# When the first scores start: eight maxima instead of eleven ahead of them

## The chip, the cores and the metric

The kernel runs on one core of a Trainium2 chip. The metric is device time in microseconds (us), the median of three runs. A core has TensorE (PE in the profile; PEld are its weight loads), VectorE (DVE), ScalarE (ACT), GpSimd (POOL) and SyncE (SP). Each works through its own queue in program order. SP issues most DMAs; ACT and POOL can issue some, and issuing takes their time.

## The reference

Input is x, 8 rows (B) of 512 tokens by 128 features, in float32. Each row is layer-normed (no learned scale) to xn. The output is x plus two things computed from xn:

- Differential attention with 8 heads. Queries and keys of each head have two halves of 8 features, values have 16. For each half: softmax of q·k / sqrt(8) over the row's 512 tokens. The second half's attention times diff_weight is taken from the first's, the result weighs the values, is rms-normed per token over all heads, scaled by norm_w, and goes through Wo; then bo and a factor 1 − diff_weight.
- A mixture of experts. A gate (xn @ Wg, sigmoid) picks 2 of 8 experts per token, with shares normed to one. Each expert is silu(xn @ We1) * (xn @ We3) @ We2 with 256 inner features; one shared expert of that kind takes all tokens. The sum is divided by 3.

## The kernel before, in words

A row is 4 tiles of 128 tokens. Its 8 heads are taken in 4 pairs (w). A pair needs first its *maxima*: for each of the two heads and each tile of queries, a product of queries and keys (L795), 128 by 1024 numbers in PSUM for the two halves together, and a reduction over them on VectorE (L802). So a pair has eight maxima. Then `shift` (L825 to 838) turns the eight maxima of each token into rows that go by DMA into the queries (`into_queries`, L820), so that the scores come out with the maximum already taken off. For the very first pair this goes through a transpose on TensorE (pm, L829), a copy on ScalarE (first_rows, L831) and two DMAs on SP.

*Scores* (L844) are the same products the other way round, with keys in the rows; ScalarE takes exp of them (L852), and `weigh` (L863) multiplies by the values, with a column of ones for the sums. Scores, maxima and weigh have a PSUM buffer each (tags "sc", "mx", "av"); only the first pair's maxima use "sc" too, by turns. Other products share three buffers (tag "mm").

The main loop has 16 steps for a row, 128 in all, plus some; a step is one pair and one tile of keys and has two turns, one for each head of the pair. A turn issues scores, then one tile of maxima (`next_maxima(1)`) for a pair to come, then at most one of the waiting DMA jobs (`copies`, `loads`, `errands`). The maxima run ahead of the scores by a fixed number of tiles: 11 are made before the loop (AHEAD), and one more is put in at the first turn, so that from there on the lead is 12. 

Everything else is cut into pieces, which generators yield with a cost in us of TensorE and a number of PSUM buffers. `pieces(step)` starts them in the first turn of a step, by due date (last step less pieces left), while the room of 2.25 us and the free buffers allow. What stands behind "soon" and "late" in a generator follows in that turn or the next. These jobs matter here:

- `norm_later(b)`: layer norm of row b (rows 0 to 2 are normed ahead of the loop): statistics on VectorE (L213 to 217), the rest on GpSimd (L218, L222).
- `gates_later`: for each row turn(b), four transposes (px, L236) and a copy to xnT (L270), then in the next piece gates(b), four products (pg, L249). Rows 0 and 1 are gated ahead of the loop. When all rows are gated, the exponential of the gates (L274) lets `route()` start, which picks experts and lists the tokens of each, in more than 20 pieces, mostly on VectorE. The experts' pieces wait for it.
- `prepare(b)`: queries and keys (pq, L727), split in an upper and a lower part (L738, L740), then values (pv, L771). The parts are copied by DMA into the places in qst and kst that the products read (L758); each such job is one entry of `copies`, two DMAs.

Ahead of the loop the order is written out by hand (L1071 to L1173): norm of row 0, the weights' transposes (pw, L1090), px of row 0, `head` for the queries and keys of the first pair (pd, L1118, without a DMA), row 0's other heads by prepare(0) and 16 DMAs, and the first eleven maxima. Between the maxima stand the gates of rows 0 and 1, and `keep_clock()` (L1149), a product of the unit matrix with xnT whose result nobody reads: ten of them. One product of 512 float32 columns is two instructions in the trace.

Of the kernel before, what the change touches and what calls it, by code (L numbers as in the profile page):

```python
# [11 lines left out]
F32 = mybir.dt.float32  # L12
# [19 lines left out]
def kernel(  # L32
# [52 lines left out]
    nc = tc.nc  # L85
    B, S, E = x.shape
    NT = S // P
    NE, _, FF = We1.shape
# [19 lines left out]
    def small_psum(name):  # L108
        return ps_3.tile([P, S], F32, tag="mm", name=name)
# [68 lines left out]
    kst = []  # L178
# [53 lines left out]
    def turn(b):  # L232

        px = small_psum(f"px_{b}")
        for t in range(NT):
            nc.tensor.transpose(px[:, t * P : (t + 1) * P], xn[b][:, t, :], ident)  # L236
        xnT = p3.tile([P, S], F32, tag="xnT", name=f"xnT_{b}")
        return xnT, px
# [4 lines left out]
    def gates(b, xnT):  # L243

        if not pgs:
            pgs.append(small_psum("pg"))
        for t in range(NT):
            i = b * NT + t
            nc.tensor.matmul(  # L249
                pgs[0][:, i * NE : (i + 1) * NE], xnT[:, t * P : (t + 1) * P], wg, start=True, stop=True  # L250
            )

    def norm_later(b):
        yield 0, 0
        yield "late"
        run(norm(b))

    def gates_later(rows):

        previous = None  # L260
        for b, ready_at in rows.items():
            while step < ready_at:
                yield 0, 0
            yield 1.35, 1
            if previous:
                gates(*previous)
            xnT, px = turn(b)
            previous = b, xnT
            yield "late"
            nc.scalar.copy(xnT, px)  # L270
        yield 0.9, 0
        gates(*previous)
        yield "late"
        nc.scalar.activation(  # L274
            gate.rearrange("p t e -> p (t e)"), pgs[0][:, : TILES * NE], AF.Exp, scale=-1.0
        )
        held.pop()
        gated.append(True)
# [266 lines left out]
    turns = 0  # L545
# [169 lines left out]
    def prepare(b):  # L715

        st = state[b]
        if "xnT" not in st:
            yield 0.45, 1
            st["xnT"], px = turn(b)  # L720
            yield "late"
            nc.scalar.copy(st["xnT"], px)
        xnT = st["xnT"]
        yield 1.75, 2
        pqs = [small_psum(f"pq_{b}_{i}") for i in range(2)]
        for i in range(2):
            nc.tensor.matmul(  # L727
                pqs[i],
                w_c[:, i].rearrange("p i f u -> p (i f u)") if b else w_rest[:, i],
                xnT,  # L730
                start=True,
                stop=True,
            )
        parts = []
        for i in range(2):
            yield ("soon", "late")[i]
            upper = p1.tile([P, S], F32R, tag=f"upper{i}", name=f"upper_{b}_{i}")
            nc.scalar.copy(upper, pqs[i])  # L738
            lower = p1.tile([P, S], F32R, tag=f"lower{i}", name=f"lower_{b}_{i}")
            nc.vector.tensor_tensor(lower, pqs[i], upper.bitcast(F32), ALU.subtract)  # L740
            parts.append((upper, lower))
        q, k = qst[b % 2], kst[b % 2]

        def no_shift():
            for half in range(2):
                nc.sync.dma_start(
                    out=q[64 * half + SHIFT : 64 * half + SHIFT + 2]
                    .bitcast(F32)
                    .rearrange("p u s -> p (u s)"),
                    in_=noughts,  # L750
                )

        def copy(part, i, s):

            row_of = (2 * part + s, part + 2 * s)[i]
            first = 0 if b else 2
            for half in range(2):
                (nc.scalar if b == 0 and i else nc.sync).dma_start(  # L758
                    out=(q, k)[i][64 * half + row_of : 64 * half + STACK : 4, first:, :].bitcast(F32),
                    in_=parts[i][part][64 * half : 64 * half + F * (H - first), :].bitcast(F32),  # L760
                )

        if b > 1:
            copies.append(no_shift)
        for part, i in ((0, 0), (0, 1), (1, 0), (1, 1)):
            for s in range(2):
                copies.append(lambda part=part, i=i, s=s: copy(part, i, s))
        yield 0.9, 1
        pv = small_psum(f"pv_{b}")
        for t in range(NT):  # L770
            nc.tensor.matmul(  # L771
                pv[:, t * P : (t + 1) * P],
                xnT[:, t * P : (t + 1) * P],
                w_t[:, 0, :],
                start=True,
                stop=True,
            )
        yield "late"
        nc.scalar.copy(
            vals[b % 2].rearrange("p t h e -> p (t h) e")[:, :, 0:DH],  # L780
            pv.rearrange("p (n e) -> p n e", e=DH),
        )
# [182 lines left out]


    STEPS = 4 * NT
    AHEAD = 11
    MIX = 30
    EACH = 4.65  # L970
    ROOM = 2.25
# [14 lines left out]
    def job(first, last, pieces, part, ready=None):  # L986

        jobs.append(Job(first, last, pieces, part, ready or (lambda: True)))

    for b in range(3, B):  # L990
        job(b - 3, b - 3, 1, norm_later(b))
    job(1, 7, 7, gates_later({b: b - 1 for b in range(2, B)}))
    job(5, 24, 22, route(), lambda: gated)
    for b in range(B):
        at = STEPS * b
        st = state[b]
        if b == 1:
            job(0, 1, 2, prepare(b))
        elif b > 1:
            job(at - 16, at - 15, 3, prepare(b))  # L1000
        job(at + 5, at + 13, 2, shared(b), lambda b=b: len(over) == b)
        job(at + 3, at + 4, 1, residual(b))
        for w in range(4):
            job(at + 4 * w + 5, at + 4 * w + 6, 1, fold(b, w), lambda st=st, w=w: ("ov", w) in st)
        job(at + 12, at + 18, 1, shared_out(b), lambda st=st: "h" in st and "r" in st)
        job(at + 17, at + 21, 2, conclude(b), lambda st=st: st.get("folds") == 4 and "r" in st)
# [55 lines left out]
    with tc.manual_schedule():  # L1062
# [3 lines left out]

        norms = {b: norm(b) for b in range(B)}
        next(norms[0])  # L1070
        rows = const.tile([P, 5], F32, name="rows")  # L1071
# [13 lines left out]
            nc.vector.tensor_scalar(signs[:, i : i + 1], lower, -2.0, 1.0, ALU.mult, ALU.add)  # L1085
        run(norms[0])

        pw = ps_1.tile([P, S], F32, tag="av", name="pw")
        for i in range(4):
            nc.tensor.transpose(pw[:, i * P : (i + 1) * P], w_raw[:, i, :], ident)  # L1090
# [51 lines left out]
            w = pw[:, i * P : (i + 1) * P]  # L1142
            nc.scalar.copy(w_c[:, i], w.rearrange("p (u i f) -> p i f u", i=2, f=F))
        nc.scalar.copy(w_t.rearrange("p i e -> p (i e)"), pw[:, 2 * P :])

        idle = ps_1.tile([P, S], F32, tag="av", name="idle")

        def keep_clock():
            nc.tensor.matmul(idle, ident, xnT, start=True, stop=True)  # L1149

        next_maxima(1)
        state[1]["xnT"], px = turn(1)
        nc.scalar.copy(state[1]["xnT"], px)
        keep_clock()
        next_maxima(1)
        run(first)
        while copies:
            copies.popleft()()
        later_constants()
        next_maxima(1)  # L1160
        gates(0, xnT)
        keep_clock()
        next_maxima(1)
        gates(1, state[1]["xnT"])
        held.append(pgs[0])
        keep_clock()
        next_maxima(1)
        keep_clock()
        next_maxima(1)
        for _ in range(AHEAD - 8):  # L1170
            keep_clock()
            next_maxima(1)
            keep_clock()  # L1173
        sides = const.tile([P, 1], F32, name="sides")
        nc.vector.memset(sides, 1.0)
# [42 lines left out]
        while step < total + 1 or jobs or errands or loads:  # L1218
            for second_half in range(2):
                if step < total:  # L1220
                    b, r = divmod(step, STEPS)
                    w, c = divmod(r, NT)
                    pe = scores(b, w, c, second_half)
                    pes = [pe] if not second_half else pes + [pe]
                if shifted:
                    shifted.popleft()()
                next_maxima(1)
                turns += 1
                if errands:

                    if latest:
                        nc.gpsimd.tensor_copy(mark, latest.pop())  # L1232
                    errands.popleft()()

                if copies and (turns % 3 or not loads):
                    copies.popleft()()
                elif loads:
                    loads.popleft()()
                if not second_half:
                    begun = pieces(step)  # L1240
                    if turns <= 1:
                        next_maxima(1)
                    follow(begun, "soon")
                else:
                    follow(begun, "late")
                    if last is not None:
                        weigh(*last)
                    if turns <= 1:
                        next_maxima(1)
                    last = (b, w, c, pes) if step < total else None  # L1250
            step += 1
# [48 lines left out]
```

## Time and profile before

| | |
|---|---|
| three runs | 671.24, 671.82, 671.85 us, median 671.82 |
| the profiled execution | 684.2 us, of which the span is 682.3 |
| TensorE busy | 625.5 us, 92% of the span |
| VectorE busy | 518.2 us, 76% |
| ScalarE busy | 357.5 us, 52% |
| mean granted TensorE clock | 0.954 |
| first scores (L844) | 46.22 us after the span's start |
| step 7 of the loop begins | 81.14 us |
| last scores | 668.55 us |

The span runs from the first to the last instruction. In an answer in order of time, a line gives start, duration, engine, line of the code, operation, what it writes and reads, and in brackets how long the engine had been idle and what released it. "SPq" and "ACTq" are DMAs issued by these engines. In an answer by stretches, a line gives the stretch, its length, then the busy time of PE, PEld, DVE, ACT and POOL, each with a count of instructions, then the granted clock of TensorE (PEclk), the busy share of the DMA engines and GB/s.

### The profile page before, as it was taken

How to read it: one execution, taken by the hardware profiler on the slowest of the kernel's cores; microseconds unless marked ns; L12 is line 12 of the kernel's file. 1: busy time of each engine (PE TensorE's matmuls, PEld its weight loads, DVE VectorE, ACT ScalarE, POOL GpSimd, SP SyncE). 2: the span in 40 equal slices, each digit the busy share in tenths (PEclk: the TensorE clock that was granted, in tenths of full speed). 3: DMA queues.
4: the chain of work that ended last, by engine and by line, in shares of the span. 5: the costliest groups of instructions: out<-in, count | busy, mean ns of one | idle time of the engine just before them, and what ended most of it. 6: DMA issues, size and time to landing. Idle time of an engine off the chain costs nothing.

```text
span 682.3 us, 10940 instructions
## 1 busy us (share of the span) xinstructions
PE 625.5 (92%) x3781; PEld 329.0 (48%) x3781; DVE 518.2 (76%) x945; ACT 357.5 (52%) x435; POOL 278.7 (41%) x455
## 2 busy tenths in 40 slices
PE   4988998789998999999999999999999999999874
PEld 1424543245543554556555554455555655555222
DVE  7658658997778787767777777867778687778983
ACT  2214543453445655566555655656466655555552
POOL 7516600048704144544544444553445425523101
PEclk9978867796989999999999999999999999999997
DMA  5222332021500233435462234435353234401360
GB/s 168 75 89 69 117 105 95 26 73 59 155 26 22 72 97 122 153 115 161 127 181 86 85 121 136 148 122 155 119 188 92 100 98 149 121 18 30 131 220 33
DMA packets 41665, 72.64 MB, mean 106 GB/s; under 512 B 10581, under 2 KB 15862, under 8 KB 41586
## 3 DMA queue, kind: packets, MB, share of 16 engines
q1 hardware_dynamic: 35978, 61.05, 28.2%
q0 software_dynamic: 4608, 9.45, 4.8%
q10 hardware_dynamic: 1024, 1.44, 0.7%
q8 instruction: 30, 0.49, 0.3%
q14 instruction: 25, 0.20, 0.1%
HBM read 46.19 MB, written 12.60 MB: 86 GB/s over the span
## 4 chain that ended last, share of the span: by engine, by line
PE 70%; DVE 21%; issue 5%; ACT 3%; POOL 0%; DVEq 0%; ACTq 0%; POOLq 0%
PE sc L844 13%; PE av L863 13%; PE mx L795 10%; DVE most L802 10%; PE ph L632 8%; PE py L645 5%; PE ps L885 3%; ACT pe L852 3%; PE ph L959 2%; PE pi L435 2%; PE po L903 2%; PE pq L727 2%; PE idle L1149 2%; PE pg L249 1%; PE pz L942 1%
## 5 line engine op out<-in xcount | busy, mean ns | idle before, releaser
L802 DVE TENSOR_REDUCE most<-mx 128x2 f32<-128x1024 f32 x256 | 312.8, 1222 | 107.4 <-PE mx L795 107.0
L852 ACT ACTIVATE pe<-sc 128x1024 f32<-128x1024 f32 x256 | 262.4, 1025 | 241.4 <-PE sc L844 239.5
L844 PE MATMUL sc<-qst,kst 64*128 64x512 f32 x512 | 131.6, 511 | 12.5 <-ACT pe L852 12.2
L863 PE MATMUL av<-pe,vals 128*32 128x512 f32 x1024 | 142.7, 630 | 0.0
L795 PE MATMUL mx<-kst,qst 64*128 64x512 f32 x512 | 123.1, 472 | 16.4 <-DVE most L802 14.5
L844 PEld LDWEIGHTS sc<-qst,kst 64*128 64x128 f32 x512 | 49.0, 188 | 157.4 <-ACT pe L852 115.7
L569 POOL DMA_INDIRECT xq<-tokens,tokens_at x72 | 71.1, 987 | 37.2 <-issue 27.0
L657 POOL DMA_INDIRECT results<-y,results_at x72 | 70.8, 984 | 36.5 <-issue 31.4
L795 PEld LDWEIGHTS mx<-kst,qst 64*128 64x128 f32 x512 | 51.4, 193 | 62.2 <-DVE most L802 50.9
L1232 POOL COPY mark<-most 1x2 f32<-1x2 f32 x144 | 25.4, 176 | 136.8 <-DVE most L802 134.2
L632 PE MATMUL ph<-xT,w 128*128 128x128 f32 x576 | 74.8, 281 | 1.0 <-DVE r L946 0.9
L632 PEld LDWEIGHTS ph<-xT,w 128*128 128x128 f32 x576 | 67.6, 191 | 9.3 <-issue 6.6
L914 POOL TENSOR_TENSOR o<-on 128x128 f32<-128x128 f32 x32 | 14.8, 462 | 137.8 <-DVE on L910 137.7
L863 PEld LDWEIGHTS av<-pe,vals 128*32 128x32 f32 x1024 | 20.6, 109 | 43.0 <-issue 42.8
L645 PE MATMUL py<-w,h 128*128 128x128 f32 x288 | 38.4, 283 | 2.8 <-DVE h L609 2.8
L645 PEld LDWEIGHTS py<-w,h 128*128 128x128 f32 x288 | 33.9, 191 | 8.0 <-issue 4.1
L606 DVE SCALAR_TENSOR_TENSOR th<-th,ph 128x512 f32<-128x512 f32 x36 | 24.6, 685 | 14.1 <-ACT th L605 14.1
L885 PE MATMUL ps<-xnT,s 128*128 128x512 f32 x64 | 32.1, 620 | 0.6 <-DVE on L910 0.6
L605 ACT ACTIVATE th<-ph 128x512 f32<-128x512 f32 x36 | 21.5, 597 | 15.6 <-PE ph L632 13.7
L873 ACT ACTIVATE ov<-av,sides 128x512 f32<-128x512 f32 x32 | 22.2, 694 | 6.8 <-PE av L863 6.5
L609 DVE TENSOR_TENSOR h<-th,ph 128x512 f32<-128x512 f32 x36 | 24.1, 669 | 0.0
L222 POOL TENSOR_SCALAR xn<-xn,both,rstd 128x128 f32<-128x128 f32 x28 | 22.0, 797 | 0.7
(161 smaller groups left out, 600.3 us busy)
## 6 DMA issues: line engine op xcount, KB each, us to landing
w<-experts SPq DMA_DIRECT2D x72, 384.0 KB
ym<-results SPq DMA_DIRECT2D x16, 256.0 KB
qst<-upper SPq DMA_DIRECT2D x28, 128.0 KB
kst<-upper SPq DMA_DIRECT2D x28, 128.0 KB
qst<-lower SPq DMA_DIRECT2D x28, 128.0 KB
kst<-lower SPq DMA_DIRECT2D x28, 128.0 KB
experts<-in_L_ffn_We_dram SPq DMA_DIRECT2D x24, 128.0 KB
r<-in_L_attn_x_dram SPq DMA_DIRECT2D x8, 256.0 KB
```

The lines of the kernel that those rows point to most:

```text
L569: nc.gpsimd.indirect_dma_start(out=xq[:, n, :], out_offset=None, in_=tokens[:, :], in_offset=bass.IndirectOffsetOnAxis(ap=tokens_at[:, j : ...
L606: nc.vector.scalar_tensor_tensor(th, th, 1.0, ph, ALU.add, ALU.mult)
L632: nc.tensor.matmul(ph[:, ns], ws[n][:, f : f + P], xT[:, ns], start=True, stop=True)
L645: nc.tensor.matmul(py[:, ns], hs[c][:, ns], ws[n][:, f : f + E], start=(c == 0), stop=(c == NF - 1))
L657: nc.gpsimd.indirect_dma_start(out=results_of[j], out_offset=bass.IndirectOffsetOnAxis(ap=results_at[:, j : j + 1], axis=0), in_=y[:, n, : ...
L795: nc.tensor.matmul(sc[:, i, :], q[ROWS[i], 2 * w + u, t * P : (t + 1) * P], k[ROWS[i], 2 * w + u, :], start=True, stop=True,)
L802: nc.vector.tensor_reduce(most[:, t, u, :], sc, AX.X, ALU.max, negate=True)
L844: nc.tensor.matmul(sc[:, i, :], kst[b % 2][ROWS[i], 2 * w + u, c * P : (c + 1) * P], qst[b % 2][ROWS[i], 2 * w + u, :], start=True, stop=True,
L852: nc.scalar.activation(pe, sc, AF.Exp, scale=F**-0.5)
L863: nc.tensor.matmul(st["av"][32 * g : 32 * g + 32, :], vals[b % 2][:, c, 2 * w + u, :], pes[u][:, i, :], start=(c == 0), stop=(c == NT - 1),)
L885: nc.tensor.matmul(ph, w[:, c * P : (c + 1) * P], st["xnT"], start=True, stop=True)
L1232: nc.gpsimd.tensor_copy(mark, latest.pop())
```

## The change

- Maxima: eight, not eleven, are made before the loop; in the loop, turns 2, 3, 4 and 6 make one more each, instead of turn 1 alone. From turn 6 on the lead is again 12.
- Unit products: ten become seven. Two come at the very start, ahead of the weights' transposes, and read a part of kst that L184 has filled with ones; one stands between maxima 5 and 6, one between 7 and 8, three after the eighth.
- Gates: row 0's move one maximum later; row 1's move into the loop's gates job, which starts at step 2 instead of 1 and takes each row two steps later than before.
- Norms of rows 3 to 7 come at steps 2 to 6 instead of 0 to 4; prepare(1) at steps 1 and 2 instead of 0 and 1.
- Of the 16 DMAs of row 0's queries and keys, the four with the keys' upper part move from ACT's queue to SP's.

```diff
@@ gates_later
             if previous:
                 gates(*previous)
+            if b in state and "xnT" in state[b]:
+                previous = b, state[b]["xnT"]
+                continue
             xnT, px = turn(b)
@@ copy, in prepare
-                (nc.scalar if b == 0 and i else nc.sync).dma_start(
+                (nc.scalar if b == 0 and i and part else nc.sync).dma_start(
@@ 
-    AHEAD = 11
+    CATCH_UP = 2, 3, 4, 6
@@ jobs
     for b in range(3, B):
-        job(b - 3, b - 3, 1, norm_later(b))
-    job(1, 7, 7, gates_later({b: b - 1 for b in range(2, B)}))
+        job(b - 1, b - 1, 1, norm_later(b))
+    job(2, 9, 8, gates_later({b: b + 1 for b in range(1, B)}))
...
         if b == 1:
-            job(0, 1, 2, prepare(b))
+            job(1, 2, 2, prepare(b))
@@ ahead of the loop
+        idle = small_psum("idle")
+        some = kst[0][:, 2, :].bitcast(F32)
+
+        def keep_clock():
+            nc.tensor.matmul(idle, ident, some, start=True, stop=True)
+
         norms = {b: norm(b) for b in range(B)}
...
         run(norms[0])
 
+        for _ in range(2):
+            keep_clock()
         pw = ps_1.tile([P, S], F32, tag="av", name="pw")
...
         idle = ps_1.tile([P, S], F32, tag="av", name="idle")
-
-        def keep_clock():
-            nc.tensor.matmul(idle, ident, xnT, start=True, stop=True)
-
+        some = xnT
         next_maxima(1)
         state[1]["xnT"], px = turn(1)
         nc.scalar.copy(state[1]["xnT"], px)
-        keep_clock()
         next_maxima(1)
         run(first)
         while copies:
             copies.popleft()()
         later_constants()
         next_maxima(1)
-        gates(0, xnT)
         keep_clock()
         next_maxima(1)
-        gates(1, state[1]["xnT"])
+        gates(0, xnT)
         held.append(pgs[0])
-        keep_clock()
         next_maxima(1)
         keep_clock()
         next_maxima(1)
-        for _ in range(AHEAD - 8):
-            keep_clock()
-            next_maxima(1)
+        for _ in range(3):
             keep_clock()
@@ main loop, in both turns
-                    if turns <= 1:
+                    if turns in CATCH_UP:
                         next_maxima(1)
```

More of the change, by code (lines that the diff above doesn't have):

```diff
@@ L1247 @@
                         weigh(*last)
-                    if turns <= 1:
+                    if turns in CATCH_UP:
                         next_maxima(1)
```

## The prediction

> **What bounds the kernel now.** I read the page's head and slices first, then the chain of waits, then the first 80 us in order of time, then busy time and clock in stretches.
>
> ```profile
> span 682.3 us, 10940 instructions
> ...
> PEclk9978867796989999999999999999999999999997
> ...
> PE 70%; DVE 21%; issue 5%; ACT 3%; POOL 0%; DVEq 0%; ACTq 0%; POOLq 0%
> ```
>
> TensorE carries 70% of the chain, VectorE 21%. So work taken off TensorE counts only where TensorE is what the next step waits for; each stretch must be asked by itself. The change touches the stretch up to step 10 of the main loop (about 0 to 100 us). In order of time, around the first scores:
>
> ```profile
> 33.43 0.49 PE L795 MATMUL mx<-kst,qst 64*128 64x512 f32 x2
> 33.96 1.23 DVE L802 TENSOR_REDUCE most<-mx 128x2 f32<-128x1024 f32 x1 [0.25 <-PE mx L795]
> ...
> 35.71 0.17 DVE L809 TENSOR_TENSOR parts<-most,parts 128x8 f32<-128x8 f32 x1
> ...
> 35.93 0.39 PE L829 MATMUL pm<-ident,parts 128*32 128x128 f32 x1 [2.01 <-DVE parts L809]
> ...
> 36.12 1.92 PE L1149 MATMUL idle<-xnT,ident 128*128 128x512 f32 x2
> 36.36 0.26 ACT L831 COPY first_rows<-pm 32x128 f32<-32x128 f32 x1 [8.43 <-DMA kst<-lower]
> 36.64 1.37 SPq L820 DMA_DIRECT2D qst<-first_rows  x2
> ...
> 38.69 3.78 PE L1149 MATMUL idle<-xnT,ident 128*128 128x512 f32 x4
> ...
> 46.22 0.49 PE L844 MATMUL sc<-qst,kst 64*128 64x512 f32 x2
> ```
>
> The eighth maximum (33.43) ends the first pair; its shift is issued on SP from 36.64 to 38.01, and in quarter-microseconds the DMA share falls to 0.03 by 39.5 before the experts' loads begin, so the first scores could run from about 39.4. They run at 46.22, behind six unit products (x2 in the trace is one product) and three more maxima in TensorE's order. That is the gap the change closes: 6.8 us.
>
> In the loop, a tile of maxima has one PSUM buffer (tag "mx"), so matmul and reduction alternate:
>
> ```profile
> 60.16 1.22 DVE L802 TENSOR_REDUCE most<-mx 128x2 f32<-128x1024 f32 x1
> ...
> 61.98 1.22 DVE L802 TENSOR_REDUCE most<-mx 128x2 f32<-128x1024 f32 x1 [0.60 <-PE mx L795]
> 63.12 0.86 DVE L213 BATCH_NORM_STATS2 stats<-xn 128x6 f32<-128x128 f32 x4
> ```
>
> One maximum costs 1.22 plus 0.60 of waiting, 1.82 us, unless other VectorE work (here a norm's 0.86 + 0.36 + 0.17 = 1.4 us) fills the wait. VectorE is busy 28.6 of the 34.9 us of steps 0 to 6: this alternation sets the pace there. Whatever the change moves into these steps is paid at VectorE's price.
>
> The clock, on a grid of 3.41 us on which its changes fall:
>
> ```profile
> core 0: us, PE busy (x) PEld busy (x) DVE busy (x) ACT busy (x) POOL busy (x), PEclk, DMA share, GB/s
> ...
> 15.17:18.59 3.42, 2.97 (x6) 1.03 (x6) 1.62 (x2) 0.13 (x1) 3.32 (x5) 1.00 0.01 2
> 18.59:22.00 3.41, 3.41 (x6) 1.42 (x7) 1.89 (x3) 1.33 (x2) 3.41 (x2) 1.00 0.00 0
> ...
> 32.24:35.65 3.41, 1.68 (x6) 0.48 (x4) 2.84 (x5) 0.00 (x0) 0.00 (x0) 0.99 0.36 114
> 35.65:39.07 3.42, 3.14 (x6) 1.20 (x7) 0.44 (x3) 0.26 (x1) 0.00 (x0) 0.50 0.19 52
> ...
> 52.72:56.13 3.41, 3.41 (x16) 2.64 (x16) 2.83 (x10) 0.00 (x0) 2.17 (x3) 0.51 0.00 0
> ```
>
> A half-busy stretch (1.68 of 3.41) is followed by half clock; a wholly busy one ends it. The clock column reads 1.00 before 35 us only because no change is recorded: four pd products take 3.75 us there, about 0.94 each, against 0.5 after 22 us.
>
> **The change, step by step.**
>
> **A. Two unit products before the weights' transposes.** They read the ones that L184 writes, ready at 4.06. At the cold rate (3.78 us for two) they hold TensorE from 4.1 to 7.9. Behind them in its queue stand the four pw transposes (1.35 us; before, done by 6.4), now done at 9.2, and px of row 0, which ran 8.25 to 9.49. VectorE's four_rest copies (8.88) need the first two transposes, there at 8.6: no wait. If the clock stays cold, px slips by 0.9 us and so does all behind it: +0.9. If it rises, the pd products and the first pq run at half the time. By the Trainium skill (TensorE: Matmul & The Clock Gate, Part 1) one fully busy window of about 3.4 us suffices; its Part 4 says against the change that transposes do not count as busy, which would leave 3.8 us of products, rarely a whole window: +0.9. The row decides: 52.72 to 56.13, which brought the clock back, holds four px transposes (1.06 us) among its busy time. So from 4.1 to about 10 us there is, mostly, a whole window, and the clock rises at some point between 8 and 12. Rise at 8.4: pd from 10.3, maximum 1 at 14.15 instead of 15.62; then 11.8 to 15.2 is only half busy, the clock falls and returns as in 18.59 to 22.00, one window earlier; maximum 3 at 20.9 for 23.26, −2.4. Rise at 11.8: 21.6, **−1.7**. I take −1.7; bounds −3.2 (never falls again) to +0.9.
>
> **B. First scores behind the eighth maximum.** Between maxima 3 and 8 go two unit products and row 1's gates (1.12 + 1.10 + 1.06); there VectorE's 1.23 per reduction takes over as pace in part. Written out from 23.26: reductions 24.6, 25.8, 27.05, 28.35, 29.95, 31.55 for 33.96: −2.4. The upper part of k moves from ACT's queue to SP's: SP issues 12 copies at 0.73, from 23.15 to 31.9, then must take the shift at 34.2: 2.3 us of room. ACT's four take 3.98 from 26.9 to 30.9, before first_rows at 33.9 (with eight it would have been 34.9: the move is needed). All copies land by about 34, before maximum 9. After pm: six products and three maxima at full clock 6 × 1.0 + 3 × 0.5, 7.6 with gaps; instead, the longer of three products (3.0) and the shift (0.30 + 1.37 + about 1.4 to land, 3.2). −4.4. At the half clock of the profile: 9.9 against 3 × 1.89 = 5.7, −4.2. B: **−6.7**, either way.
>
> **C. Paid back in the loop.** Three more maxima in steps 0 to 2 (extra at turns 2, 3, 4, 6 for turn 1), written out with 1.02 for exp, 0.5 per product: reductions 9 to 18 end at 2.3, 4.1, 5.9, 7.7, 10.2, 12.2, 14.1, 16.0, 18.2 and 20.8 after the first scores (prepare's two lower parts 1.4, parts 0.9 and one norm in between), the nineteenth at 22.6. The same place before: 65.59 − 46.22 less 0.65 for the cold stretch at 53 to 56, 18.75. +3.85. Two norms that were done by then are not: 2 × (1.4 − 0.6 + 0.1 of gaps), +1.8. C: **+5.65**. Row 1's gates (1.06 of TensorE) lie under the alternation of steps 3 to 6, where TensorE has idle time; without that cover +1.06. VectorE's 0.8 us of sides and keep, in the loop's way at 46.45, now lie under the shift's flight; counted above.
>
> **D. Gates, row 1's queries, routing.** The planner's first gate piece with row 1 runs at step 4 and the last at step 10 instead of 8; routing starts and ends two steps later (30 instead of 28), the first expert at step 35 instead of 33. Two steps lose routing's VectorE work early and two gain it late; experts run three to five steps behind their dates anyway and the last ends near step 115, with nothing waiting until 118. Row 1's copies at steps 1 to 6 have until step 10. 0, bounds −1 to +1.
>
> **Sum:** −1.7 − 6.7 + 5.65 = −2.75. The profiled execution, 684.2 (682.3 span and 1.9 around it), would become 681.4. It is 12.4 above the median; it holds about 55 us of half clock before 200 us, so I carry the difference, not the level, to the median: 671.82 − 2.75 = **669.1**.
>
> **Rivals.**
> 1. *Slower: the clock falls in step 0.* The first 4.65 us after the new first scores have 2.5 us of products, 54%; the row at 32.24 fell at 49%. From there pq (2.0) and pv (1.06) double. One window costs up to 1.7 us where TensorE is the pace; from the second on the gain is gone. The profile has five in a row (80 to 97 us, each fully busy yet half clock); four would give −2.75 + 6.8 = +4, 675.9. Against: steps 1 and 2 have about 80% of work, and the kernel before risks the same (it fell at 52.7).
> 2. *No difference:* the early products only delay (A = +0.9) or C reaches 7: 671.8, within 1.3.
> 3. *Larger:* the clock stays up from 8 us (A = −3.2) and the extra maxima fill idle VectorE time. Counted by VectorE's idle time: from reduction 3 (24.59) to step 7 (81.14) it is busy 39.9 of 56.55 us; of the 16.6 idle, 2.3 (six products and three maxima at half clock) + 0.65 come from the clock, which leaves 13.7. After: 0.9 between reductions 3 and 8, 3.9 until reduction 9, nine unfilled waits of 0.6: 10.2. B and C give −3.5, with A −6.7: 665.1.
>
> **How the numbers follow.** 0.2% of the median, 1.3 us, is about what a measurement can tell from no change. Likeliest 0.45 (667.5 to 670.5); larger 0.12; none 0.20; slower 0.23. The first, but for 0.01, and the second are faster: 0.56; same 0.21; slower 0.23. The range goes from 665.0 to 676.0, taking in rival 1 to four windows.
>
> **What would show it.** Right: the first scores at 37 to 40 us; pd products at half their 0.94 before 16 us; reductions 10 to 18 at 1.82 apart; step 7 only two to four us earlier than its 81.1. Wrong: pd still 0.94 (A), SP issuing copies past 34 (B), PEclk 0.50 in steps 0 to 3 (rival 1), experts late past step 115 (D).

## The result, and the profile after

The changed kernel takes **678.99 us** (median of 4 runs, 678.57 to 682.60), the kernel before 671.84 us on the same chip (4 runs, 671.24 to 673.61): a ratio of 1.0114, 95% interval 1.0075 to 1.0153. Run again beside 51 executions of the kernel before, it gives 1.0139 (1.0071 to 1.0206). So it is slower by 7 to 9 us in the medians (6.7 in the mean over all executions, by the table further down). The forecast was 669.1, with 665.0 to 676.0 as its range.

The two profiled executions do not show this difference: 684.2 before and 679.0 after. That of before was 12 us above its own median and that of after on it, so the traces can be compared place by place, not by their totals. Ratios, here and below, leave out executions more than 1.5% above the fastest of their kernel; medians and means keep them.

The page of the changed kernel, head, clock and chain:

```profile
span 676.8 us, 10923 instructions
...
PE 613.4 (91%) x3775; PEld 324.8 (48%) x3775; DVE 518.2 (77%) x945; ACT 357.0 (53%) x435; POOL 278.6 (41%) x455
...
PEclk9886798978999999999979999999999999999899
...
PE 70%; DVE 23%; ACT 3%; issue 2%; POOL 1%; DMA 0%; DVEq 0%; ACTq 0%
```

The chain is divided as before, TensorE 70%. The clock row is uneven in its first ten slices, as before; the 7 in slice 21, about 340 us, has no counterpart there.

The changed kernel in order of time, up to the first scores:

```profile
4.20 3.47 PE L1077 MATMUL idle<-kst,ident 128*128 128x512 f32 x4 [4.20 <-DVE stats L213]
7.51 0.60 PE L1102 MATMUL pw<-ident,w_raw 128*128 128x128 f32 x4
...
10.06 1.95 PE L1130 MATMUL pd<-xnT,four_rest 128*128 128x512 f32 x4 [0.72 <-ACT xnT L1118]
...
18.37 0.49 PE L798 MATMUL mx<-kst,qst 64*128 64x512 f32 x2
...
25.52 0.49 PE L798 MATMUL mx<-kst,qst 64*128 64x512 f32 x2
26.72 2.79 SPq L761 DMA_DIRECT2D qst<-lower  x4
28.12 0.37 PE L832 MATMUL pm<-ident,parts 128*32 128x128 f32 x1 [2.11 <-DVE sides L1178]
28.29 4.17 PE L1077 MATMUL idle<-xnT,ident 128*128 128x512 f32 x6
29.62 1.35 SPq L823 DMA_DIRECT2D qst<-first_rows  x2
32.39 0.50 PE L847 MATMUL sc<-qst,kst 64*128 64x512 f32 x2
```

What the change does ahead of the loop, it does. The first scores run at 32.39 for 46.22. Two instructions of pd take 0.98 us instead of 1.88, and SP had issued the last of its twelve copies at 29.51, a tenth of a microsecond before the shift at 29.62.

The reductions on VectorE behind that, then both kernels in the stretch that holds the loop's first steps, and some of the clock's own windows. In each trace all recorded changes of the clock lie whole multiples of 3.41 us apart; in this one they fall on 7.27, 27.75, 31.16, 37.99 and so on, so the windows are cut there:

```profile
33.20 1.23 DVE L805 TENSOR_REDUCE most<-mx 128x2 f32<-128x1024 f32 x1 [4.43 <-PE mx L798]
35.02 1.23 DVE L805 TENSOR_REDUCE most<-mx 128x2 f32<-128x1024 f32 x1 [0.59 <-PE mx L798]
36.84 1.23 DVE L805 TENSOR_REDUCE most<-mx 128x2 f32<-128x1024 f32 x1 [0.60 <-PE mx L798]
```

Before:

```profile
core 0: us, PE busy (x) PEld busy (x) DVE busy (x) ACT busy (x) POOL busy (x), PEclk, DMA share, GB/s
32.00:83.00 51.00, 43.89 (x208) 20.12 (x207) 35.64 (x89) 19.98 (x25) 25.68 (x37) 0.87 0.30 91
```

After:

```profile
core 0: us, PE busy (x) PEld busy (x) DVE busy (x) ACT busy (x) POOL busy (x), PEclk, DMA share, GB/s
3.86:7.27 3.41, 3.07 (x4) 1.40 (x5) 3.24 (x17) 0.25 (x2) 3.29 (x4) 1.00 0.87 254
...
32.00:83.00 51.00, 41.03 (x198) 19.36 (x196) 34.43 (x79) 20.39 (x24) 22.56 (x28) 0.77 0.33 103
...
34.58:37.99 3.41, 1.13 (x6) 0.39 (x6) 2.37 (x2) 1.93 (x2) 0.00 (x0) 1.00 0.68 203
37.99:41.40 3.41, 3.28 (x5) 1.46 (x6) 1.30 (x2) 0.51 (x2) 0.00 (x0) 0.50 0.46 143
...
328.00:336.00 8.00, 7.76 (x52) 3.72 (x50) 5.97 (x9) 5.28 (x8) 3.44 (x7) 1.00 0.50 159
336.00:340.00 4.00, 0.00 (x0) 0.00 (x0) 1.64 (x7) 0.88 (x1) 1.42 (x2) 0.80 0.28 83
340.00:344.00 4.00, 3.80 (x14) 3.09 (x15) 1.23 (x1) 0.41 (x1) 0.47 (x2) 0.50 0.76 217
```

Reductions 9, 10 and 11 are 1.82 apart, as forecast. But of the 51 us, TensorE spends 23 at half clock (0.77) instead of 13 (0.87): in the loop it begins behind a window with 1.13 us of products in 3.41. Of the lead of 13.8 us at the first scores, 5.3 are left at step 7 (75.80 for 81.11).

The other place is far away, at 336 us, in step 58 of the loop: four microseconds in which TensorE does nothing, then half clock. In order of time there, TensorE, SP and the last step of the rows on VectorE:

```profile
329.40 0.37 SPq L592 DMA_DIRECT2D w<-experts  x1
329.82 1.34 SPq L761 DMA_DIRECT2D kst<-lower  x2
335.26 0.50 PE L847 MATMUL sc<-qst,kst 64*128 64x512 f32 x2
336.33 0.21 DVE L838 STREAM_TRANSPOSE rows<-parts 128x32 f32<-128x32 f32 x1
336.57 0.53 SPq L840 DMA_DIRECT2D turned<-rows  x1
337.15 1.27 SPq L761 DMA_DIRECT2D kst<-lower  x2
340.20 1.35 PE L798 MATMUL mx<-kst,qst 64*128 64x512 f32 x2 [4.44 <-DMA kst<-lower]
```

In the view of waits it is one wait, with the total, the number and the longest:

```profile
PE mx L798 <- DMA kst<-lower: 4.4, 1, 4.4
```

SP issues its last entry before the gap at 329.8 to 331.2, and the next at 336.57: it stands at `turned<-rows`, a DMA of the rows of a pair's maxima, until VectorE has made these rows (336.54). Row 4's last copy of keys stands behind it in the queue, leaves at 337.15 and lands when TensorE has waited 4.4 us for it. Before, in the same place:

```profile
337.32 1.25 SPq L758 DMA_DIRECT2D kst<-lower  x2
...
340.88 1.34 SPq L758 DMA_DIRECT2D kst<-lower  x2
...
347.85 0.53 SPq L837 DMA_DIRECT2D turned<-rows  x1
```

All copies go first, and nothing waits. Through this place the lead of the changed kernel, 11.3 us at step 58, falls to 4.9 at step 60. From step 96 on the two traces run in step, 4.1 to 5.0 apart: what is left at the end was decided in the first 60 steps.

### The profile page after: what moved, and what is told of

The parts are those of the page before. It is cut to its first block, busy times and chain, and to the rows that moved or that the text cites. A ratio compares the mean times of both kernels' runs of the same rounds, so it can differ in the third digit from the quotient of the medians.

```text
span 676.8 us, 10923 instructions
## 1 busy us (share of the span) xinstructions
PE 613.4 (91%) x3775; PEld 324.8 (48%) x3775; DVE 518.2 (77%) x945; ACT 357.0 (53%) x435; POOL 278.6 (41%) x455
## 3 DMA queue, kind: packets, MB, share of 16 engines
q10 hardware_dynamic: 800, 1.05, 0.5%
## 4 chain that ended last, share of the span: by engine, by line
PE 70%; DVE 23%; ACT 3%; issue 2%; POOL 1%; DMA 0%; DVEq 0%; ACTq 0%
PE sc L847 13%; PE av L866 13%; DVE most L805 11%; PE mx L798 11%; PE ph L635 9%; PE py L648 5%; PE ps L888 4%; PE pi L438 3%; ACT pe L855 2%; PE po L906 2%; PE ph L962 2%; PE pq L730 2%; PE pxq L621 1%; DVE what L459 1%; DVE parts L812 1%
## 5 line engine op out<-in xcount | busy, mean ns | idle before, releaser
L635 PE MATMUL ph<-xT,w 128*128 128x128 f32 x576 | 76.9, 287 | 0.4 <-DVE r L949 0.4
L635 PEld LDWEIGHTS ph<-xT,w 128*128 128x128 f32 x576 | 69.2, 195 | 9.7 <-issue 7.8
L866 PEld LDWEIGHTS av<-pe,vals 128*32 128x32 f32 x1024 | 20.7, 110 | 44.7 <-issue 44.5
L609 DVE SCALAR_TENSOR_TENSOR th<-th,ph 128x512 f32<-128x512 f32 x36 | 24.6, 685 | 14.2 <-ACT th L608 14.0
L906 PE MATMUL po<-ident,ov 128*128 128x128 f32 x128 | 20.3, 282 | 3.0 <-DVE lower L743 2.1
```

The lines of the kernel that those rows point to most:

```text
L635: nc.tensor.matmul(ph[:, ns], ws[n][:, f : f + P], xT[:, ns], start=True, stop=True)
L866: nc.tensor.matmul(st["av"][32 * g : 32 * g + 32, :], vals[b % 2][:, c, 2 * w + u, :], pes[u][:, i, :], start=(c == 0), stop=(c == NT - 1),)
L906: nc.tensor.transpose(po[:, t * P : (t + 1) * P], ov[:, t * P : (t + 1) * P], ident)
```

## The experiments

Two theories stood against each other at first. D: the later dates (norms, prepare(1), gates and routing) are the loss, through the stall at step 58 and what else they bring. P: the new work ahead of the loop and the maxima put into its first steps are the loss, through the clock. In the expectations of the first runs the stall alone is called theory S, and P is called rival C.

**The kernel before, once more** (no edit), to see how much the profiled execution of one kernel varies:

> The kernel before, unchanged, for a profile that stands near its median of 671.8 us. Both theories: about 672 us. What is asked of it: where its first scores come when the clock is not in the way (the prediction took 43.9 us) and how far it leads or trails the changed kernel at step 58, where the changed kernel stands at 335.3 us.

678.7 us, first scores at 44.9 us instead of 46.22. The same kernel gave 671.8 and 684.2: executions differ by more than the change does, and the traces differ in the time at half clock. What follows rests on many executions (4 to 22 of each edited kernel, against 33 to 51 of the kernel before on the same chip).

**The later dates alone**, on the kernel before (with the change's lines in `gates_later`, so that row 1 is taken there):

```diff
     for b in range(3, B):
-        job(b - 3, b - 3, 1, norm_later(b))
-    job(1, 7, 7, gates_later({b: b - 1 for b in range(2, B)}))
+        job(b - 1, b - 1, 1, norm_later(b))
+    job(2, 9, 8, gates_later({b: b + 1 for b in range(1, B)}))
...
-            job(0, 1, 2, prepare(b))
+            job(1, 2, 2, prepare(b))
...
-        gates(1, state[1]["xnT"])
```

> The kernel before with the later dates alone (norms of rows 3 to 7, gates with row 1, prepare of row 1, routing); eleven maxima and ten unit products as before. Theory S (the loss is the stall of 4.4 us at step 58, where the last copy of row 4's keys stands behind a waiting DMA on SP, and the later dates put it there): the same stall appears, plus the clock it costs, so 677 to 680. Rival C (the loss comes from the prologue: three maxima paid back at more than they gained, and a colder clock): 671 to 673, for the prologue is the old one.

688.7 us (only 4 executions), ratio 1.0207 (1.0132 to 1.0282), with a wait of 4.5 us for row 4's keys: against C, and more than the 677 to 680 of S. The dates alone lose more than the whole change, so they carry the loss.

**The stall taken away, and made.** On the changed kernel two waiting copies instead of one go at turn 115, ahead of the DMA that waits for its rows. On the kernel before, turn 115 issues none, so that the last copy falls behind that DMA.

```diff
                     copies.popleft()()
+                    if turns == 115:
+                        copies.popleft()()
```

```diff
-                if copies and (turns % 3 or not loads):
+                if copies and (turns % 3 or not loads) and turns != 115:
                     copies.popleft()()
```

> The changed kernel with one edit: at turn 115 two copy jobs are issued instead of one, so that the last copy of row 4's keys goes ahead of the rows of maxima on SP. Theory S: no wait for that copy near 336 us, 671 to 674. Rival C: 678 to 680 as the changed kernel, since the prologue is unchanged. The prediction's own sum of parts A to C would be 669.

> The kernel before with one edit: no copy job at turn 115, so that the last copy of row 4's keys is issued at turn 116, behind the rows of maxima on SP. Theory S: a wait of about 4 us appears near step 58, 676 to 679. Rival C: 671 to 673.

The first gives 676.02 us, ratio 1.0038 (1.0011 to 1.0065), between what S and what C expected: the stall is a part of the loss, not all of it. The copies leave together, and no wait follows; in order of time:

```profile
336.34 2.66 SPq L761 DMA_DIRECT2D kst<-lower  x4
...
340.63 0.39 PE L798 MATMUL mx<-kst,qst 64*128 64x512 f32 x2
```

The second gives 679.61, ratio 1.0087 (1.0064 to 1.0110), a little above S's range, and the wait is there in a kernel that has no other part of the change:

```profile
337.05 0.61 SPq L837 DMA_DIRECT2D turned<-rows  x1
337.71 1.30 SPq L758 DMA_DIRECT2D kst<-lower  x2
...
340.69 0.76 PE L795 MATMUL mx<-kst,qst 64*128 64x512 f32 x1 [4.45 <-DMA kst<-lower]
```

One pair of DMAs on the wrong side of one waiting DMA costs 0.87%, 5.8 us: more than the 4.45 of the wait. In all four traces with the stall 6.8 us of half clock follow within steps 56 to 62, and in none of the 13 traces without it is there any in these steps.

**All of the change except the dates** (the changed kernel with the old ones), and the changed kernel again beside it:

```diff
-        job(b - 1, b - 1, 1, norm_later(b))
-    job(2, 9, 8, gates_later({b: b + 1 for b in range(1, B)}))
+        job(b - 3, b - 3, 1, norm_later(b))
+    job(1, 7, 7, gates_later({b: b - 1 for b in range(2, B)}))
...
-            job(1, 2, 2, prepare(b))
+            job(0, 1, 2, prepare(b))
...
         gates(0, xnT)
+        gates(1, state[1]["xnT"])
```

> The changed kernel with the old dates: norms, gates with row 1's ahead of the loop, prepare of row 1 and so routing as before; prologue, unit products and catch-up as changed. Theory D (the later dates alone bring the loss: a stall of 6.6 us at step 58 and some 25 us more of half clock before step 57, about 9 us): the prologue's gain stays, 663 to 668. Rival P (the half clock comes from the prologue with fewer unit products and the catch-up turns): only the stall is gone, 671 to 676. The prediction's sum of A to C: 669.

> The changed kernel, unchanged, on the same chip as the others of this call, since single executions of one kernel spread by several us. Both theories: 677 to 680.

671.43 us, ratio 0.9947 (0.9915 to 0.9978), and 682.43, ratio 1.0139 (1.0071 to 1.0206), somewhat more than expected. Without the later dates the change is faster than the kernel before: by 0.53% in the ratio, by 0.27% (1.8 us) in the medians, by 2.3 us in the mean over all executions. None of the other runs is clearly better. The median lies in what P expected and the gain is smaller than D's, but its sign is D's.

**The dates without the stall** (the dates alone, with two copies at turn 115), and **the change without the early products** (the old-dates kernel without them):

```diff
                     copies.popleft()()
+                    if turns == 115:
+                        copies.popleft()()
```

```diff
-        for _ in range(2):
-            keep_clock()
```

> The kernel before with the later dates, and two copy jobs at turn 115 so that the stall of step 58 is gone. Theory D: the half clock is still there, 679 to 683. Rival P: nothing is left of the loss, 671 to 674.

> As the changed kernel with the old dates, but without the two unit products ahead of the weights' transposes. It tells what part A is worth. The prediction (A = -1.7, bounds -3.2 to +0.9): 1.7 us slower than with them. The first trace of the changed kernel (first scores at 32.4 us, 5 us earlier than the prediction's 37 less A) lets A be as large as -5: then 5 us slower. If the products only delay: 1 us faster.

680.42, ratio 1.0076 (1.0047 to 1.0106), as D expected: without the stall the dates still lose. And 674.13, ratio 1.0014 (0.9978 to 1.0050): without the two early products nothing is left of the old-dates kernel's gain. They are worth 0.67% by the ratios, but only 2.7 us in the medians and 2.3 in the means; the expectation from part A was 1.7. First scores, catching up and the rest together are not measurably different from no change in total time (at equal clock, further down, they gain 1.6 us). In order of time without them:

```profile
10.21 3.75 PE L1128 MATMUL pd<-xnT,four_rest 128*128 128x512 f32 x4 [0.72 <-DVE both L215]
...
23.25 0.50 PE L798 MATMUL mx<-kst,qst 64*128 64x512 f32 x2
...
37.19 0.97 PE L847 MATMUL sc<-qst,kst 64*128 64x512 f32 x2 [0.67 <-DMA qst<-first_rows]
```

pd is back at 0.94 each and the third maximum at 23.25 us instead of 18.37; the first scores come at 37.19.

**Which dates?** Norms (by one step) and prepare(1) later, and gates and routing later without the stall, each on the kernel before:

```diff
-        job(b - 3, b - 3, 1, norm_later(b))
+        job(b - 2, b - 2, 1, norm_later(b))
-            job(0, 1, 2, prepare(b))
+            job(1, 2, 2, prepare(b))
```

```diff
-    job(1, 7, 7, gates_later({b: b - 1 for b in range(2, B)}))
+    job(3, 9, 7, gates_later({b: b + 1 for b in range(2, B)}))
...
+                    if turns == 115:
+                        copies.popleft()()
```

> The kernel before with norms of rows 3 to 7 one step later and prepare of row 1 one step later, gates and routing as before. If the gates' and routing's dates alone carry the remaining 5 us of the later dates: no difference, 672 to 674.5. If VectorE's norms or row 1's queries carry it: 676 to 679.

> The kernel before with the gates of rows 2 to 7 two steps later, and so routing, norms and prepare as before; two copy jobs at turn 115, so that there is no stall at step 58. If gates and routing carry the remaining 5 us: 677 to 680. If norms or prepare carry it: 672 to 674.5.

677.98, ratio 1.0067 (1.0038 to 1.0096), and 679.38, ratio 1.0050 (1.0022 to 1.0078). Each median lies in the range that blames its own dates: both lose, about alike, and no single date is to blame. The first has row 4's copies ahead of the waiting DMA without help, so the stall belongs to gates and routing. The order of instructions on SP's queue says the same (T14 to T16: the DMA of a pair's rows; Q, K: copies of row 4's queries and keys, u and l for upper and lower part, two DMAs each; w: experts' weights; i, r, N: others):

```
before:        w i w w N Qu r Qu Ku T14 | w i Ku Ql w Ql Kl w Kl T15 | w i w w w w T16
later dates:   w i w w r N Qu T14 | Qu i Ku Ku w Ql Ql w Kl T15 | Kl i w w w w w T16
```

With later routing the first expert starts at step 36.2 instead of 34.3, prepare(4) begins one step later (51.2 instead of 50.2), and its last entry (Kl) passes to the other side of T15.

**Is it the clock?** In the later-dates kernels TensorE has more time at half clock, so products of the unit matrix were put into steps 10 to 31, where a PSUM buffer was free (19 products of two times 256 columns in the dates kernel, 18 in the old-dates kernel), and for comparison into steps 0 to 3 only. There a buffer was free in steps 2 and 3 alone, so that run has two products more, not four:

```diff
                 begun.append(j)
+            if 10 <= step < 32 and banks > 0:
+                spare = small_psum(f"spare_{step}")
+                for i, s in enumerate((s1, s3)):
+                    nc.tensor.matmul(spare[:, i * FF : (i + 1) * FF], ident, s, start=True, stop=True)
             return begun
```

> As the dates without the stall (680.4), with one more unit product (about 1 us of TensorE) in each of steps 10 to 31 that has a PSUM buffer to spare, 19 in all. Theory clock (the remaining 5 us are half clock that gaps of TensorE in routing's steps bring): the clock stays up there, 674 to 677 although there is more work. Theory work (the later routing itself costs time on VectorE or TensorE): 680 to 690.

> The changed prologue with the old dates (671.4), with the same unit products in steps 10 to 31, 18 in all. If half clock in routing's steps costs more than the products: 664 to 670, and better than both kernels. If not: 672 to 682.

> The changed prologue with the old dates (671.4, 48 us of half clock on average), with one unit product in each of steps 0 to 3. If TensorE's gaps between the catch-up maxima bring the half clock: 10 us less of it, at 0.3 us each, less the products that do not fit in gaps: 667 to 670. If not: 672 to 675.

689.2, ratio 1.0240 (1.0206 to 1.0273); 682.16, ratio 1.0127 (1.0083 to 1.0170); 671.74, ratio 0.9968 (0.9940 to 0.9996). The many products cost far more than they save. The two, between their two expectations, make no difference that can be told from the old-dates kernel, and TensorE's gaps in steps 0 and 1 stay untested.

**Fewer maxima at once, and a product between the first maxima.** Both on the old-dates kernel:

```diff
-    CATCH_UP = 2, 3, 4, 6
+    CATCH_UP = 2, 4, 7, 10
```

```diff
         nc.scalar.copy(state[1]["xnT"], px)
+        keep_clock()
         next_maxima(1)
```

> The changed prologue with the old dates, the extra maxima at turns 2, 4, 7 and 10 instead of 2, 3, 4 and 6. If the gaps of crowded maxima bring the half clock or the alternation costs more when crowded: 667 to 670. If each extra maximum costs its 1.8 us wherever it stands: 671 to 673.

> The changed prologue with the old dates, with the unit product after the third maximum as in the kernel before. If the prologue's gaps bring the half clock at about 26 to 33 us: 668 to 671. If they do not, the product only delays by up to 1 us: 671.5 to 673.

675.18, ratio 0.9989 (0.9958 to 1.0021), and 674.11, ratio 0.9938 (0.9894 to 0.9983). Both medians lie above what either side expected. Spreading the extra maxima does not help, so there is no sign that their crowding in steps 1 to 3 costs clock. The product is worth nothing that can be told from the old-dates kernel.

**All executions together.** Each execution has its span and mean granted clock; the time at half clock is twice (1 − clock) times the span. The 179 executions of the kernel before spread from 20 to 67 us of half clock (their means on the four chips of the experiments lie within 1 us), and over all 397 executions a straight line with one slope and one level for each kernel fits with a residual of 1.9 us (standard deviation): **0.30 us (± 0.01) for each microsecond at half clock**. Fitted one by one, the larger groups give 0.20 to 0.36, so a level that is carried over 20 us of half clock may be off by 1 to 2 us. With that reserve the line separates what a kernel does at equal clock from what the clock does to it:

| kernel | executions | half clock, mean us (standard error) | level to before at equal half clock, us | mean time to before, us |
|---|---|---|---|---|
| before | 179 | 39.3 (0.8) | 0 | 0 |
| changed | 10 | 62.8 (2.7) | −0.3 (0.7) | +6.7 |
| dates only | 4 | 69.4 (10) | +7.2 (1.0) | +16.1 |
| changed, no stall | 22 | 58.6 (2.2) | −4.5 (0.5) | +1.2 |
| before, with the stall | 20 | 42.9 (1.9) | +4.5 (0.5) | +5.6 |
| old dates | 22 | 48.1 (2.1) | −5.0 (0.4) | −2.3 |
| dates only, no stall | 22 | 55.3 (3.5) | +1.7 (0.5) | +6.5 |
| old dates, no early products | 14 | 44.7 (2.3) | −1.6 (0.5) | 0.0 |
| norms, prepare(1) later | 12 | 45.7 (1.5) | +0.6 (0.6) | +2.5 |
| gates, routing later | 22 | 45.6 (2.2) | +0.6 (0.4) | +2.5 |
| dates, no stall, 19 products | 6 | 42.4 (2.8) | +13.3 (0.8) | +14.2 |
| old dates, 18 products | 6 | 38.7 (4.1) | +5.9 (0.8) | +5.7 |
| old dates, two products | 22 | 43.4 (2.1) | −3.6 (0.4) | −2.4 |
| old dates, maxima spread | 22 | 55.3 (3.1) | −4.0 (0.5) | +0.8 |
| old dates, one product | 14 | 45.3 (3.5) | −3.4 (0.5) | −1.6 |

By this table the changed kernel's +6.7 us are: −5.0 for everything ahead of the dates; +0.5 for the dates at equal clock (no stall, against old dates); +4.2 for the stall (changed, against no stall); and 23.5 us more of half clock, which at 0.30 make +7.0. Of these 23.5, about 9 are there with the old dates, 10.5 come with the later dates and 4 with the stall (each ± 2 to 3). The 18 or 19 products took 9 and 13 us of half clock away (± 4.5), worth 2.8 to 3.9 us, and cost 11 to 12 us at equal clock.

## Why the prediction was wrong

**D is the step that failed.** It set gates, row 1's queries and routing at nothing, within 1 us. Its reason, that later routing is repaid before anything waits for the last expert, held: steps 28 to 32 take 24.0 us with the later dates for 21.0, steps 32 to 56 114.7 for 117.7, and the level at equal clock moves by 0.5 to 1.7 us. What it left out is another's place in a queue. It asked when row 1's copies are needed, and not what else the planner would move when the experts come later. Row 4's pieces move by a step, and its last copy of keys, which still had slack of its own, falls behind a DMA that waits for its rows. Taken away and made alone, that is 4.2 to 4.5 us at equal clock and 5.5 us in the means; neither the price nor the place was in the sum or in a rival. In ratios: with the old dates 0.9947, with the later ones but no stall 1.0038, with the stall 1.0114 to 1.0139. In the means D is 9.0 us instead of 0 (from −2.3 to +6.7): 5.5 are the stall with its half clock, and of the other 3.5 about 3 are more half clock.

**Rival 1 was right in kind and too narrow in place.** Half clock did take the gain, at 0.77 in the loop's first 51 us. It was put into step 0 alone, with up to four windows; in the changed kernel it sets in once before the first scores (27.75 us), then in steps 1, 2, 3, 6, 14, 18, 22, 30, 58 and 120, the same in both of its profiled executions. Its price was set higher than it is: I counted up to 1.7 us for a window of 3.41, the line says 0.30 × 3.41 = 1.0. The chance of 0.23 was too low in part because the dates were never asked what they do to the clock.

**A was right in sign and too small.** The early products take 3.47 us, not 3.78, and the transposes behind them run at 0.15 each: the trace's first clock record, full clock, is at 7.27, sooner than the 8.4 of the early case, and the window before it (3.86 to 7.27) holds 3.07 us of the early products and nothing else. So the Trainium skill's rule that one busy window suffices (TensorE: Matmul & The Clock Gate, Part 1) agrees with this trace, with a window nine tenths full, and the objection from its Part 4 was not put to the test. The clock also stayed up until 27.75, and the third maximum came 4.9 us earlier, where I had 1.7 and a bound of 3.2. In time at equal clock A is worth −3.4 (with and without the early products), at the bound; in the mean over all executions, −2.3. One reading beside it was off: in the trace of before, full clock is on record from 21.95, so only up to there does the column read 1.00 for want of a record.

**B and C were near.** First scores come at 32.39, 13.8 us earlier in the profile for a forecast of 8.4, and before the 37 to 40 that were named as a sign. Of the 5.4 us more, A's clock has 3.2; without the early products, B alone brings them from 46.22 to 37.19, 9.0 for 6.7. Reductions 18 and 19 end 22.15 and 23.97 us after the first scores, for 20.8 and 22.6: C is 1.4 us short, with two windows of half clock on the way. B and C together are −1.6 at equal clock for a forecast of −1.05. SP's room ahead of the shift, 2.3 us by forecast, was 0.1.

A to C together were put at −2.75 and measure −5.0 at equal clock, or −2.3 with the half clock that they bring; a forecast for the old-dates kernel would have held, but partly by luck: the 1.7 us by which A was put too small and the 2.6 us of half clock, which were not in the sum, work against each other.

**What stays open** is why the earlier start and the later dates bring more half clock. The traces say where: in steps 10 to 32, six of the seven with later gates and routing have 20.5 us of it (the seventh 44.4), and the ten with the old ones 3.4 to 27.3, 12.3 on average (one trace each). They also say behind what: windows in which TensorE has half its time without products (counted at the end). That is an observation beside it, not a cause shown: two products in steps 2 and 3, spreading the maxima and a product in the prologue moved the half clock by −5, +7 and −3 us, none by more than twice its error, and only filling steps 10 to 31 lowered it by two to three times its error, at a price that hides any gain.

## What to carry to other kernels

When a step of a planned schedule moves, list the queue of every engine again around all that depends on it, hundreds of microseconds later too: a DMA that must wait for its data holds up every DMA behind it, however early those are ready. Such a fault costs a line to mend once it is seen (two copies in one turn), so look in the view of waits for the one wait that is new before judging a change by its total. Where executions of one kernel differ by more than the change, read each beside its clock: the level at equal clock and the time at half clock are two results.

## What the runs showed of the hardware

- In these kernels a microsecond at half clock costs 0.30 us; were TensorE the pace all the time, it would be 0.5. The 43 executions of the kernel before in one series lie between 667.7 and 684.7 us, and about three quarters of their variance follow the clock (squared correlation 0.78).
- The clock of a cold TensorE rose at 7.27 us, after 3.07 us of back-to-back products from 4.20 on. The two products for it are worth 2.3 us in the mean over all executions and 3.4 at equal clock.
- Cut into windows of 3.41 us at their own changes of the clock, the 17 traces show what goes before a change. Of 113 windows at full clock with at most 1.9 us of products, 100 were followed by half clock (1.73 us in the window of before that ends at 35.60, with no gap over 1.7); of 380 with 1.9 to 2.8 us, 41; of 2552 fuller ones, 3. So an engine need not be idle for a whole window. At half clock none of the 66 windows with less than 2.9 us was followed by full clock, but 127 of 183 fuller ones were.
- A DMA queue stood behind one DMA that waited for its data: from 331.2 to 336.57 us SP issued nothing, though a copy that was ready stood next, and TensorE waited 4.4 us for that copy. In the run with two copies at turn 115 it left without a wait, with the one before it.
